# q and k parts stored once and doubled by a zero stride in the load; maxima without a lead of three buffers

## The chip, the cores and the metric

One core of one Trainium2 chip. The metric is the device time of one execution in microseconds (us); lower is better. The engines are named as in the profile: PE (matrix products; PEld is its weight load), DVE (vector), ACT (activation functions), POOL (GpSimd) and SP (the queue that issues most transfers). Transfers are issued by SP and ACT and carried by 16 DMA engines.

## The reference

The input is x of 8 batches x 1024 tokens x 256 features, float32. Three residual steps follow one another: half a mixture-of-experts layer, a causal attention of 16 heads of 16 features, and again half a mixture-of-experts layer.

```python
x = x + 0.5 * ffn(layernorm(x))
x = x + attn(layernorm(x))
x = x + 0.5 * ffn(layernorm(x))

# attn: q, k, v = projections of x with biases, 16 heads of 16
dots = einsum('bhid,bhjd->bhij', q * hd**-0.5, k)
dots = where(causal, -1e9, dots)
out = softmax(dots) @ v          # then @ Wo.T + bo

# ffn: two experts of 8 a token; an expert with more than cap = 1280 choices is dropped whole
keep = counts <= cap
```

An expert that more than 1280 of the 16384 choices fall on gives nothing. The kernel counts the choices, and runs the experts only where one is kept. In the executions shown none is: the profile is the attention with the routing's choices around it.

## The kernel before, in words

**Units.** The attention works in 32 units: 8 batches (`b`) x 4 groups of 4 heads (`g`). A unit's q and k lie in one of three tiles `qks[u % 3]`, of 128 rows: two heads of 64 rows each, for q and k (`t`) and for two pairs of heads (`pr`), 1024 tokens wide.

**Parts.** For float32 accuracy with products of a reduced type each head's q and k are split into a high and a low part of 16 rows. A head's 64 rows of q are high, low, high, low, those of k high, high, low, low, so one product of 64 rows sums all four combinations. `project(b, gp)` (lines 740 to 766) makes the parts for 8 heads: products `pq`, then on ACT `whole` and `high`, on POOL `low`, for each half of the tokens and for q and k. The tiles `high` and `low` have three buffers each. SP stores them into the DRAM tile `parts`; `fetch(u)` (lines 769 to 779) loads them from there into `qks`, for unit u + 2 while unit u runs. A batch has 8 such pairs of tiles.

**Maxima and scores.** `m_steps(u)` has 18 steps a unit, M: a product of q and k into PSUM (`sm`), and on DVE the row maxima (`mx`). They are needed before the scores. When all maxima of a half (`hf`) of the queries are there, `settle` turns them on DVE (`mxr`, `mneg`, `mside`), and `send` passes them through DRAM with two transfers of ACT's queue: `rows<-mside`, and after that has landed `neg<-rows`. `e_steps(u)` has 18 steps a unit, E: a product that starts with minus the maxima (`sc<-neg,take_m`), then k and q (`sc<-qk`), and ACT's exponential (`pT`). The first 5 E of a unit are of the first half of the queries, the other 13 of the second. POOL masks, and products with the values (`pav`) follow some steps later; their result is copied by ACT (`att`), and SP stores it (`sums<-att`), in the middle of the unit for the first half and a few steps into the next unit for the second. `sm` and `sc` share three pairs of PSUM banks.

**Order.** Every engine's instructions keep the order of the source (line 623 records each operation, so all have this line in the profile). A unit is 36 steps, E and M in turn: E of unit u, M of the units after it. A counter `count` tells the steps; `start(steps, lag)` (line 1229) puts work into `timed`, due `(3 * lag + 2) // 4` steps later, and `due()` runs it ahead of the step. So `fetch(u + 2, lag=6)`, started with a lag of 8, issues at steps 6, 11, 16 and 21 of unit u; `send` issues `rows` 2 steps after the last maxima of a half and `neg` 5 steps after that. In unit 1 three M are put ahead of the first E (lines 1307 to 1309), so from then on maxima run three M (six steps) ahead: the last M of a unit's own successor is done at step 29, and M at steps 31, 33 and 35 are already those of the unit after that. Between the steps `gap` lays in projections, values, the output product and the rest.

**Transfers.** Eight semaphores tell of the landings of all transfers of SP and ACT, by turns: in the built program each transfer waits for the landing of the eighth before it.

Of the kernel before, what the change touches and what calls it, by code (L numbers as in the profile page):

```python
# [10 lines left out]
F32 = mybir.dt.float32  # L11
# [18 lines left out]
def macaron_kernel(  # L30
# [24 lines left out]
    HD = D // NH  # L55
# [543 lines left out]
    def attention(run_no, src, dst, gate0, logits, tally):  # L599
# [4 lines left out]
        with stack:  # L604
# [134 lines left out]

            def project(b, gp):  # L740
                xnT = xnTs[b]
                parts = parts_d[b, gp] = passing.tile([2, 8, 4, HD, S], F32, tag=f"parts{gp}", name=f"parts{b}_{gp}")
                for s0 in range(0, S, 512):
                    for t, (wT, bT, scale) in enumerate(((wqT, bqT, QSCALE), (wkT, bkT, 1.0))):
                        pq = bank(f"pq{b}_{gp}_{s0}_{t}")
                        for o in (0, 256):
                            for c in range(DC):
                                product(
                                    pq[:, o : o + 256],
                                    wT[:, c, gp * P : (gp + 1) * P],  # L750
                                    xnT[:, c, s0 + o : s0 + o + 256],
                                    start=(c == 0),
                                    stop=(c == DC - 1),
                                )
                                if (c, o) != (DC - 1, 256):
                                    yield
                        whole = ap.tile([P, 512], F32, tag="whole", name=f"whole{b}_{gp}_{s0}_{t}")
                        high = ap.tile([P, 512], F32R, tag="high", name=f"high{b}_{gp}_{s0}_{t}", bufs=3)
                        low = ap.tile([P, 512], F32R, tag="low", name=f"low{b}_{gp}_{s0}_{t}", bufs=3)
                        on.scalar.activation(whole, pq, AF.Identity, bias=bT[:, gp : gp + 1], scale=scale)  # L760
                        on.scalar.copy(high, whole)
                        on.gpsimd.tensor_tensor(low.bitcast(F32), whole, high.bitcast(F32), ALU.subtract)
                        for c in range(4):
                            part = (high, low)[c // 2 if t else c % 2]
                            on.sync.dma_start(out=parts[t, :, c, :, s0 : s0 + 512], in_=part.bitcast(F32))
                        yield True


            def fetch(u, s0=0, w=S, lag=8):
                b, g = divmod(u, NG)  # L770
                gp, k = divmod(g, 2)
                for pr in range(2):
                    for t in range(2):
                        h = 4 * k + 2 * pr
                        on.sync.dma_start(
                            out=qks[u % 3][:, t, pr, s0 : s0 + w].bitcast(F32),
                            in_=parts_d[b, gp][t, h : h + 2].rearrange("h c d s -> (h c d) s")[:, s0 : s0 + w],
                        )
                        yield lag


# [49 lines left out]
            def m_steps(u):  # L831
# [56 lines left out]
                def settle(hf):  # L888
                    mx = ap.tile([P, 4, 2, 2], F32, tag="mxr", name=f"mxr{u}_{hf}")
                    on.vector.tensor_reduce(  # L890
                        mx.rearrange("p x b a -> p x a b"),
                        mx_tiles[u % 3][hf].rearrange("p h r (a b) s -> p (h r) a b s", a=2),
                        AX.X,
                        ALU.max,
                    )
                    yield
                    mx = mx.rearrange("p (h r) b a -> p h (r b a)", h=2)
                    neg = ap.tile([P, 2, 2, 8], F32R, tag="mneg", name=f"mneg{u}_{hf}")
                    high, low = neg[:, :, 0], neg[:, :, 1]
                    on.vector.tensor_scalar(high, mx, -1.0, None, ALU.mult)  # L900
                    yield
                    on.vector.scalar_tensor_tensor(
                        low.bitcast(F32), mx, -1.0, high.bitcast(F32), ALU.mult, ALU.subtract
                    )
                    yield
                    turned = ap.tile([P, 32], F32, tag="mside", name=f"mside{u}_{hf}")
                    on.vector.transpose(turned, neg.bitcast(F32).rearrange("p x c i -> p (x c i)"))
                    start(send(hf, turned), 3)
                    yield

                def send(hf, turned):
                    rows = passing.tile([8, 512], F32, tag="rows", name=f"rows{u}_{hf}")
                    on.scalar.dma_start(out=rows.rearrange("c (i s q) -> s c i q", i=4, s=4), in_=turned)
                    yield 6
                    on.scalar.dma_start(
                        out=negs[u % 2][hf][62:66, :, :512].bitcast(F32),
                        in_=rows.rearrange("(p r) s -> p r s", r=2),
                    )
# [310 lines left out]
            def start(steps, lag=0):  # L1229
                timed.append([count[0] + (3 * lag + 2) // 4, steps])  # L1230
# [29 lines left out]
            for u in range(-1, NU):  # L1260
                b, g = divmod(u, NG)
                rate, every = 17 / 12, FILLS
                if u < 0:
                    rate, every = 23 / 9, 2
                elif g == 0:
                    spare[0] = False
                    if b == 0:
                        work.append(project(0, 1))
                        rate = 8 / 3
                    if b + 1 < B:  # L1270
                        work += [enter(b + 1), project(b + 1, 0)]
                        if b:
                            work.append(leave(b - 1))
                        work += [project(b + 1, 1), values_of(b + 1)]
                    if b:
                        start(divide(b - 1, 1, 0), 4)
                        after[u - 1, 1] = divide(b - 1, 1, 1)
                    side.append(gate_first(b))
                elif g == 1 and b + 1 == B:
                    work.append(leave(b - 1))  # L1280
                elif g == 2:
                    if b + 2 < B:
                        start(read(b + 2), 24)
                    if b + 1 == B:
                        start(divide(b, 0, 0), 12)
                        start(divide(b, 0, 1), 16)
                        after[u, 0] = divide(b, 1, 0, 4, (8, 1, 6, 8))
                elif g == 3:
                    if b + 1 < B:
                        start(divide(b, 0, 0), 8)  # L1290
                        start(divide(b, 0, 1), 20)
                    if b + 2 < B:
                        side.appendleft(prepare(b + 2))
                    if b + 1 == B:
                        after[u - 1, 1] = divide(b, 1, 1, 4, (6, 1, 4, 5))
                        last_on.append(ap.tile([P, 4, P], F32, tag="wsb", name="last_on", bufs=4))
                        on.gpsimd.memset(last_on[0], 0.0)
                        rate = 8 / 3
                if u == 0:
                    start(fetch(2, lag=5), 26)  # L1300
                elif u >= 0 and u + 2 < NU:
                    start(fetch(u + 2, lag=6), 8)
                if u < 0:
                    for _ in range(18):
                        step(maxima, every, rate, 1)
                else:
                    if u == 1:
                        for n in range(3):
                            step(maxima, every, rate, n)
                    es = deque(e_steps(u))  # L1310
                    for k, which in enumerate("EMEMEM" * 6):
                        small = 3 if k % 6 in (1, 5) else 0
                        if which == "E":
                            step(es.popleft(), 2 if u + 1 == NU else every, rate, 0 if u + 1 < NU else 2)
                        elif stream[0] < 18 * NU:
                            step(maxima, every, rate, small)
                if u < 0:
                    while 0 not in bases:
                        take(work)
                elif g == NG - 1:  # L1320
                    while work and u + 1 < NU:
                        drain(work.popleft())
# [75 lines left out]
```

## Time and profile before

| what | value |
|---|---|
| median of 3 runs | 1232.97 us (1225.27 to 1233.84) |
| the profiled execution's own time | 1243.32 us |
| its span | 1241.2 us |
| PE, DVE, ACT, POOL busy | 92%, 76%, 60%, 35% |
| PE busy in 96 to 1168 us | 1033.7 of 1072 us |
| DMA moved | 190.25 MB, mean 153 GB/s |
| loads `qk<-parts` | 124 of 512 KB, 8 of 256 KB |
| stores `parts<-high`, `parts<-low` | 128 and 128 of 256 KB |
| `rows<-mside`, `neg<-rows` (ACT's queue) | 64 and 64 of 16 KB |

The span is that of one profiled execution; its own time lies 10.3 us above the median of the runs. The page gives busy times of each engine, the DMA queues, the chain of work that ended last and the costliest groups of instructions. "Idle" is told with what ended it; "issue" in the chain is time for which the profile shows no wait. The table of windows gives, for a stretch, the busy time of each engine, the granted clock of PE, the mean busy share of the 16 DMA engines and GB/s.

### The profile page before, as it was taken

The page shows a single profiled execution, that of the slowest core. Times are in us where ns is not written, and L with a number is a line of the kernel's source. Part 1 is how long each engine was busy: PE and PEld are TensorE (multiplying, and loading weights), DVE is VectorE, ACT ScalarE, POOL GpSimd, SP SyncE. Part 2 cuts the span into 40 slices and gives each one's busy share as a digit, 9 for nine tenths or more (in the row PEclk, how much of TensorE's full clock was granted, in tenths as well). Part 3 has the DMA queues.
Part 4 walks back from the last instruction along what each step waited for, and adds up shares of the span by engine and source line. Part 5 has one row for each costly group of instructions (what it writes and reads, how often), then busy time and mean ns, then how long its engine had stood idle before and what let it go on. Part 6 is the DMA issues. An engine that isn't in the chain of part 4 may idle for free.

```text
span 1241.2 us, 36200 instructions
## 1 busy us (share of the span) xinstructions
PE 1143.7 (92%) x15178; PEld 668.6 (54%) x15178; DVE 939.9 (76%) x1649; ACT 739.6 (60%) x955; POOL 434.8 (35%) x773
## 2 busy tenths in 40 slices
PE   4698999999999998999899998999989999999982
PEld 2455555555565554655456555655546555555541
DVE  2487668878698777888688787988778886798923
ACT  3155676666576565675566655765656655665650
POOL 2434233343344233442334433342344413232331
PEclk9698999999899998999999999999999999999997
DMA  3634674363555545353653635555553545543201
GB/s 108 234 123 167 208 224 130 119 231 105 189 153 158 187 153 189 119 182 134 214 168 112 221 112 194 148 161 189 164 192 113 185 137 182 156 126 105 83 19 38
DMA packets 108501, 190.25 MB, mean 153 GB/s; under 512 B 24736, under 2 KB 42280, under 8 KB 108328
## 3 DMA queue, kind: packets, MB, share of 16 engines
q1 hardware_dynamic: 96776, 184.54, 45.6%
q10 hardware_dynamic: 11552, 3.29, 1.2%
q8 instruction: 122, 2.00, 0.6%
q14 instruction: 51, 0.42, 0.1%
HBM read 94.50 MB, written 93.31 MB: 151 GB/s over the span
## 4 chain that ended last, share of the span: by engine, by line
PE 79%; DVE 10%; DMA 4%; issue 3%; ACT 2%; POOL 1%; ACTq 0%; SPq 0%; POOLq 0%; DVEq 0%
PE sc L623 23%; PE pav L623 21%; PE sm L623 16%; PE pq L623 8%; DVE mx L623 7%; PE px L623 4%; PE pv L623 4%; DMA rows<-mside 3%; PE pta L623 2%; ACT pT L623 1%; DMA parts<-low 1%; DVE mneg L623 0%; DVE st_a L623 0%; DVE xn_a L623 0%; DMA qk<-parts 0%
## 5 line engine op out<-in xcount | busy, mean ns | idle before, releaser
L623 DVE TENSOR_REDUCE mx<-sm 128x2 f32<-128x1024 f32 (+2 forms) x576 | 685.2, 1216 | 211.9 <-PE sm L623 186.0
L623 ACT ACTIVATE pT<-sc 128x1024 f32<-128x1024 f32 x576 | 575.0, 1023 | 329.7 <-PE sc L623 284.6
L623 POOL TENSOR_SCALAR_AFFINE_SELECT pT<-pT 128x256 f32<-128x256 f32 (+1 forms) x448 | 190.7, 440 | 496.0 <-ACT pT L623 485.4
L623 PE MATMUL pav<-pT,vaug 128*32 128x256 f32 (+3 forms) x4608 | 325.8, 390 | 1.4 <-ACT att L623 1.4
L623 PE MATMUL sm<-qk 64*128 64x512 f32 (+3 forms) x1536 | 266.9, 385 | 38.3 <-issue 20.7
L623 PE MATMUL sc<-neg,take_m 64*128 64x512 f32 x1152 | 266.8, 459 | 6.9 <-DVE mx L623 3.5
L623 PE MATMUL sc<-qk 64*128 64x512 f32 (+3 forms) x1536 | 230.9, 337 | 0.0
L623 PEld LDWEIGHTS sm<-qk 64*128 64x128 f32 x1536 | 142.1, 189 | 139.1 <-issue 69.8
L623 PEld LDWEIGHTS pav<-pT,vaug 128*32 128x32 f32 x4608 | 113.6, 109 | 103.4 <-issue 54.7
L623 PEld LDWEIGHTS sc<-neg,take_m 64*128 64x128 f32 x1152 | 110.5, 188 | 100.4 <-issue 50.3
L623 PEld LDWEIGHTS sc<-qk 64*128 64x128 f32 x1536 | 147.6, 188 | 16.5
L623 POOL TENSOR_TENSOR low<-whole,high 128x512 f32<-128x512 f32 x64 | 82.0, 1281 | 157.1 <-ACT high L623 146.2
L623 PE MATMUL sm<-masked,before_k 64*128 64x128 bf16 (+1 forms) x1280 | 87.2, 215 | 0.0
L623 PE MATMUL pq<-xnT,wkT 128*32 128x256 f32 x1024 | 75.7, 405 | 0.0
L623 PE MATMUL px<-woT,on 128*32 128x264 f32 x1024 | 73.7, 387 | 0.9 <-ACT on L623 0.9
L623 PE MATMUL pv<-wvT,xnT 128*32 128x264 f32 x1024 | 74.0, 391 | 0.0
L623 PE MATMUL pq<-xnT,wqT 128*32 128x256 f32 x1024 | 72.7, 389 | 0.5 <-ACT xnT L623 0.5
L623 PEld LDWEIGHTS <-before_k 64*128 64x128 bf16 x1280 | 38.3, 97 | 43.8 <-issue 27.5
L623 POOL TENSOR_TENSOR x_a<-x_a,bo_all 128x512 f32<-128x512 f32 x32 | 41.5, 1301 | 57.5 <-DVE xn_a L623 36.5
L623 PE MATMUL pta<-ident,xn_a 128*32 128x128 f32 (+1 forms) x912 | 33.9, 278 | 18.3 <-DVE xn_a L623 18.1
L623 PEld LDWEIGHTS pq<-xnT,wkT 128*32 128x32 f32 x1024 | 34.4, 115 | 28.0 <-issue 10.8
L623 PEld LDWEIGHTS pq<-xnT,wqT 128*32 128x32 f32 x1024 | 33.2, 112 | 27.8 <-issue 10.8
(128 smaller groups left out, 734.3 us busy)
## 6 DMA issues: line engine op xcount, KB each, us to landing
qk<-parts SPq DMA_DIRECT2D x124, 512.0 KB
parts<-high SPq DMA_DIRECT2D x128, 256.0 KB
parts<-low SPq DMA_DIRECT2D x128, 256.0 KB
sums<-att SPq DMA_DIRECT2D x62, 256.0 KB
x_a<-in_L_attn_x_dram SPq DMA_DIRECT2D x16, 512.0 KB
out_dram<-x_a SPq DMA_DIRECT2D x16, 512.0 KB
on<-sums SPq DMA_DIRECT2D x30, 256.0 KB
rs<-inv SPq DMA_DIRECT2D x30, 256.0 KB
```

The lines of the kernel that those rows point to most:

```text
L623: i = call(*args, **kwargs)
```

## The change

Three things change. The DRAM tile `parts` holds each head's high and low part once (32 rows a head, not 64). A load reads them twice by a stride of zero: for q the 32 rows (high, low of a feature side by side) as a block twice over, for k each of the 32 rows twice in a row; a load takes one head, so there are 8 loads a unit, two at each of the four steps. And the three M ahead in unit 1 go, with shorter lags of `send` for the last unit.

```diff
-                parts = parts_d[b, gp] = passing.tile([2, 8, 4, HD, S], F32, ...)
+                parts = parts_d[b, gp] = passing.tile([2, 8, 2 * HD, S], F32, ...)
...
-                        for c in range(4):
-                            part = (high, low)[c // 2 if t else c % 2]
-                            on.sync.dma_start(out=parts[t, :, c, :, s0 : s0 + 512], in_=part.bitcast(F32))
+                        form = ("h (d c) s -> c h d s", "h (c d) s -> c h d s")[t]
+                        for c, part in enumerate((high, low)):
+                            on.sync.dma_start(
+                                out=parts[t].rearrange(form, c=2)[c, :, :, s0 : s0 + 512], in_=part.bitcast(F32)
+                            )
...
                 for pr in range(2):
                     for t in range(2):
-                        h = 4 * k + 2 * pr
-                        on.sync.dma_start(
-                            out=qks[u % 3][:, t, pr, s0 : s0 + w].bitcast(F32),
-                            in_=parts_d[b, gp][t, h : h + 2].rearrange("h c d s -> (h c d) s")[:, s0 : s0 + w],
-                        )
+                        for h in range(2):
+                            rows = parts_d[b, gp][t, 4 * k + 2 * pr + h][:, s0 : s0 + w]
+                            on.sync.dma_start(
+                                out=qks[u % 3][64 * h : 64 * h + 64, t, pr, s0 : s0 + w].bitcast(F32),
+                                in_=rows.unsqueeze(t).to_broadcast([2 * HD, 2, w] if t else [2, 2 * HD, w]),
+                            )
                         yield lag
...
-                    start(send(hf, turned), 3)
+                    start(send(hf, turned), 3 if u + 1 < NU else 1)
...
-                    yield 6
+                    yield 6 if u + 1 < NU else 4
...
-                    if u == 1:
-                        for n in range(3):
-                            step(maxima, every, rate, n)
```

In the built program a store of q has 128 rows at one stride and 512 elements (before: 8, 16 and 512), one of k still 8, 16 and 512. A load of q reads 2 (stride zero), 32 and 1024 elements, one of k 32, 2 (stride zero) and 1024, both into 64 rows of the tile.

More of the change, by code (lines that the diff above doesn't have):

```diff
@@ L741, in project @@
                 xnT = xnTs[b]
-                parts = parts_d[b, gp] = passing.tile([2, 8, 4, HD, S], F32, tag=f"parts{gp}", name=f"parts{b}_{gp}")
+                parts = parts_d[b, gp] = passing.tile([2, 8, 2 * HD, S], F32, tag=f"parts{gp}", name=f"parts{b}_{gp}")
                 for s0 in range(0, S, 512):
```

## The prediction

> **What bounds the kernel now.** I read the page first: which engine is full, and what the chain that ended last is made of.
>
> ```profile
> PE 1143.7 (92%) x15178; PEld 668.6 (54%) x15178; DVE 939.9 (76%) x1649; ACT 739.6 (60%) x955; POOL 434.8 (35%) x773
> ...
> q1 hardware_dynamic: 96776, 184.54, 45.6%
> ...
> PE 79%; DVE 10%; DMA 4%; issue 3%; ACT 2%; POOL 1%; ACTq 0%; SPq 0%; POOLq 0%; DVEq 0%
> ```
>
> PE is busy 92% of the span and is 79% of the chain. The 16 DMA engines are half idle on average; as long as transfers land in time they cost nothing. So the change, which moves only transfers and the order of maxima, can cost or gain only where PE waits for a transfer. Next, how many of the 16 DMA engines one transfer uses: the table of windows (busy times, granted clock, busy share of the DMA engines, GB/s), in a stretch that holds stores of parts alone and one that holds loads of 128 rows.
>
> ```profile
> 28.50:30.50 2.00, 0.58 (x12) 0.09 (x4) 0.00 (x0) 1.02 (x3) 1.26 (x1) 1.00 0.51 183
> ...
> 57.00:61.00 4.00, 3.93 (x50) 1.65 (x46) 4.00 (x4) 0.88 (x4) 1.31 (x3) 1.00 0.99 383
> ```
>
> With several stores queued, 0.51 of the engines work: eight. Such a store's pattern in DRAM is 8 heads, 16 rows, 512 elements. With loads whose slowest dimension is 128 rows, all 16 work, at 383/(0.99 x 16) = 24.2 GB/s each; over the whole span the page gives 184.54 MB/(0.456 x 16 x 1241.2 us) = 20.4. The number of engines follows the slowest dimension of a pattern.
>
> Then the timeline of one unit, from its first score (PE) to the first score that reads the second half's maxima, and two of ACT's pairs of transfers.
>
> ```profile
> 291.01 0.50 PE L623 MATMUL sc<-neg,take_m 64*128 64x512 f32 x2
> ...
> 296.73 0.32 SPq L623 DMA_DIRECT2D sums<-att  x1
> ...
> 297.62 1.72 SPq L623 DMA_DIRECT2D qk<-parts  x2
> ...
> 300.23 0.40 PE L623 MATMUL sc<-neg,take_m 64*128 64x512 f32 x2
> ```
> ```profile
> 321.20 0.53 ACTq L623 DMA_DIRECT2D rows<-mside  x1
> ...
> 330.36 0.63 ACTq L623 DMA_DIRECT2D neg<-rows  x1
> ...
> 340.60 0.54 ACTq L623 DMA_DIRECT2D rows<-mside  x1
> ...
> 345.55 0.65 ACTq L623 DMA_DIRECT2D neg<-rows  x1
> ```
>
> SP issues the next loads as soon as the sums that wait for att are out, 6 to 8 us into the unit; the score that needs the second half's neg comes 9.2 us into it. The transfer neg cannot be issued before rows has landed. From the increments of each transfer's semaphore in the trace, rows lands in 1.9 us when nothing of SP is outstanding, 6.6 us after 321.20 with six of SP's transfers ahead; neg in 2.1 us, and 4.6 to 6.4 us with five ahead. It lands just before the last of those that SP issued ahead of it: ACT's transfers queue behind SP's and overtake about one.
>
> Last, the chain in order of time shows the one place where a load is late today.
>
> ```profile
> 323.37 1.03 ACT pT L623
> 324.40 1.91 issue
> 326.31 0.93 PE sm L623 x6
> ```
>
> PE stands until a maximum of the unit after next gets its q and k (that load lands at 326.2). The same step recurs at 470.15 (2.64), 615.17 (2.78), 759.77 (2.39), 903.50 (2.64) and 1048.47 (1.10): 13.5 us in all. It comes back every 144.5 us, four units of 36 steps each: 36.1 us a unit, about 1 us a step.
>
> **The change, part by part.**
>
> *Stores.* Each projection tile is stored with 2 transfers, not 4: 128 instead of 256 of 256 KB, 33.5 MB less. Those of q now have 128 equal rows (16 engines), those of k still 8 heads. SP saves 128 issues of some 0.6 us and pays 132 more of 0.46 us for the loads; SP waits most of the time, so both count nothing.
>
> *Loads.* A unit has 8 of 256 KB, not 4 of 512 KB, issued in pairs at the same four steps (6, 11, 16, 21). Those of k have slowest dimension 32 in the source, 64 in the tile: 16 engines, 0.7 us, as before. Those of q read [2 copies, 32 rows, 1024]. No row shows a slowest dimension of 2. Bounds: all 16 engines, 262144 B/(16 x 24.2) = 0.7 us; or two engines, 131072 B/24.2 = 5.4 us each. The nearest row is the store (8 of 8), so I take two engines: a pair of q occupies them for 10.8 us, and every other transfer that has a share on these two waits.
>
> The Trainium skill, DMA: Bandwidth & Descriptors, section Rules for kernel authors, says that an outermost zero-stride broadcast of c copies confines a DMA to at most c engines, and speaks against just this pattern; by it the load takes the 5.4 us, and the opposite end would need it to be wrong. The window with 0.51 agrees with it for a count of 8; no row here shows 2.
>
> Is there room? On the busiest two engines: q loads 33.5 MB/2 = 16.8 MB; k loads 2.1, stores 1.05 + 2.1, sums 1.0, on and rs 2.0, x in and out 1.05, small ones 0.4: 26.5 MB. At 24.2 GB/s 1096 us, at 20.4 1300 us; the stretch that carries loads lasts some 1140 us. They are full, or just over: queues of 5 to 15 us behind each pair.
>
> *Who waits: neg of the second half.* Without the lead the last maximum of a unit comes 6 steps later, so its rows goes out at step 2 of the next unit and its neg at step 7, where it went out at step 1. SP's pair of q, issued at 6 to 7 us, is then just ahead of it; it is needed at 9.2 us. Lower bound, overtaking all: issue 7.3 + 2.1 = 9.4, a wait of 0.2 us. Upper bound, behind both q: 6.5 + 10.8 + 1 = 18, less one overtaken transfer at most: a wait of 7 us. I take 3 us (one q of 5.4 overtaken, one not: landing near 12.3). PE's queue is in order, so maxima, values and projections behind that score stand too. 31 units x 3 = +93 us.
>
> *Who waits: ACT for rows of the first half.* Its rows goes out at step 16, with the second pair of q, and its neg is queued on ACT at step 21: ACT stands until rows has landed, and behind it the exponentials, for which PE waits after some 3 steps (three pairs of PSUM). Rows of 2 us: nothing. Rows of 9 to 10 us, behind both q: ACT stands 4.5 us, PE 2.5. I take 1 us x 31 = +31 us.
>
> *The lead.* The maxima of unit u+2 start at step 37 after the step counter's zero of unit u, not 31; the last load goes out at 21. Even at 10 us a pair q and k are there by 36. The 13.5 us above go: between 0 and -13.5, I take -10. If the q loads were later by another 5 us, this cover would be gone and the wait would come back as 1 to 5 us a unit.
>
> *Start and end.* At the start the first maxima wait for POOL's memset until 53 us, but the loads of units 0 and 1 now put 4 x 2.7 x 2 + 4 x 5.4 = 43 us on two engines, with rows of unit 0 behind them: 0 to +20, I take +10. In the last unit no maxima lie between the scores; lags shortened by 2 each: 0 to +8, I take +2.
>
> Sum: 93 + 31 - 10 + 10 + 2 = +126. The profiled execution's own time was 1243.3 us (span 1241.2), 10.3 above the median of 1233.0 of the runs shown. 1243.3 + 126 - 10.3 = **1359 us**.
>
> **Rivals.** (a) ACT's transfers interleave with SP's packet by packet: neg is late by 0.5 us, rows (32 small packets an engine between packets of 4 KB) still blocks ACT for about a microsecond: 31 x 1.5 - 13 + 8 + 2 = +44, 1277 us. For it: some neg land at 2.1 us with one transfer ahead. Against it: 4.6 to 6.4 with five. The same page of the Trainium skill, section Queues, rings and completion order, has the engines take turns between the queues of SP and ACT at every packet; by it the sum would be this one, by the rows here it is nearer the next, and the measured 6.4 us decides for me.
> (b) Strict order: 7 + 2.5 us a unit, 31 x 9.5 - 13 + 20 + 4 = +306, 1538 us. For it: six transfers ahead and 6.6 us. Against: the last one is mostly overtaken, and as PE stands the next pair comes later, which thins the queue.
> (c) Faster: the repeated copies are spread over 16 engines after all. Then a q load lands in under 3 us, 33.5 MB less are written, the 13.5 us go, and the waits for rows on the chain (2.8% of the span, 35 us) shrink by a third: 1243.3 - 13 - 12 - 10.3 = 1208 us. It decides as soon as a pair of q takes under about 3 us. For it only that no row shows the pattern; against it the window with 0.51.
> (d) No change: neg and q arrive within the idle time there is, since 8% of PE is idle; but of its 97.5 us 29.2 lie ahead of 96 us and 30.0 after 1168 us, by windows over these stretches; the 1072 us between have 38.3, in hundreds of small gaps.
>
> **How the numbers follow.** Forecast 0.46, (a) 0.24, (b) 0.20, (c) 0.05, (d) 0.05. A measurement of this kernel tells about 1% from no change. Faster by over 1% is (c): 0.05; within 1% (d): 0.05; slower the rest: 0.90. The forecast's own range is 1300 to 1430 (1 to 5 us a unit around its terms); with (a) below and most of the way to (b) above, 1255 to 1520.
>
> **What would show it.** Right: in a stretch with q loads alone the share of DMA engines is near 2/16; scores of the second half wait for neg (PE or its weight load ahead of sc, idle of some us once a unit); neg on ACT issued over 5 us after rows; the waits of 1.9 to 2.8 us of sm gone. Wrong: a pair of q landing within 3 us; PE at 92% or more; or PE waiting chiefly for qk (loads later than I have them) or ACT for high (stores holding its three buffers).

## The result and the profile after

| | before | after |
|---|---|---|
| median (6 runs each, same chip) | 1233.4 us (1225.3 to 1237.2) | 1427.5 us (1420.9 to 1431.7) |
| profiled execution, its span | 1243.3, 1241.2 us | 1425.8, 1424.0 us |
| PE busy, PE idle within the span | 1143.7, 97.5 us | 1212.1, 211.9 us |
| mean granted clock of PE | 0.964 | 0.917 |

The changed kernel takes 1.158 times as long, 95% interval 1.153 to 1.163: slower, as forecast, by 195 us where the forecast had 126. The page of the profile after, with the lines that answer to those shown of before:

```profile
span 1424.0 us, 36302 instructions
...
PE 1212.1 (85%) x15178; PEld 702.3 (49%) x15178; DVE 937.4 (66%) x1649; ACT 738.2 (52%) x955; POOL 433.4 (30%) x773
...
q1 hardware_dynamic: 80144, 150.99, 34.3%
...
PE 50%; DMA 31%; DVE 9%; issue 3%; ACT 2%; SPq 2%; POOL 1%; ACTq 1%; POOLq 0%; DVEq 0%
DMA qk<-parts 15%; PE sc L623 15%; PE pav L623 14%; PE sm L623 9%; DMA neg<-rows 9%; DVE mx L623 5%; PE pq L623 5%; DMA rows<-mside 3%; PE pv L623 3%; PE px L623 2%; DMA parts<-low 2%; DMA rs<-inv 2%; SPq L623 2%; ACT pT L623 2%; PE pta L623 1%
```

33.5 MB less pass through q1 and the transfers are busy for a smaller share, yet DMA is now 31% of the chain that ended last; it was 4%. The chain goes through the loads `qk` (15%) and `neg` (9%). What PE waits for (line, what ended the wait, us in total, times, longest):

```profile
PE sc L623 <- DMA neg<-rows: 79.9, 22, 6.1
PE sm L623 <- ACT pT L623: 33.4, 12, 5.4
PE sc L623 <- DVE mx L623: 20.7, 14, 7.5
PE sm L623 <- DMA qk<-parts: 18.7, 6, 8.7
...
PE sm L623 <- issue: 5.9, 2, 3.5
```

In before the same answer has 3.5 us for `mx`, and:

```profile
PE sm L623 <- issue: 20.7, 7, 4.1
...
PE sm L623 <- DMA qk<-parts: 12.3, 3, 10.7
...
PE sm L623 <- ACT pT L623: 4.5, 4, 2.1
...
PE sc L623 <- DMA neg<-rows: 1.7, 1, 1.7
```

Now one unit in the timeline of after (start, duration, engine, and in brackets the idle time with what ended it). The unit starts at 506.1.

```profile
507.81 0.53 ACTq L623 DMA_DIRECT2D rows<-mside  x1
...
511.93 0.49 PE L623 MATMUL sc<-neg,take_m 64*128 64x512 f32 x2
...
512.12 0.34 SPq L623 DMA_DIRECT2D sums<-att  x1
...
512.55 2.48 SPq L623 DMA_DIRECT2D qk<-parts  x4
...
512.88 0.63 ACTq L623 DMA_DIRECT2D neg<-rows  x1
...
521.38 0.80 PE L623 MATMUL sc<-neg,take_m 64*128 64x512 f32 x2 [5.73 <-DMA neg<-rows]
```

SP issues q, q, k, k behind `sums`; ACT issues `neg` 0.33 us after the first of them. By the increments of its semaphore `neg` lands at 521.25, 8.4 us after its issue, where it takes 2.1 alone; the two loads of q land at 523.3 and 528.2. PE starts 0.13 us after `neg`, 5.73 us late, and its two products of that line then take 0.80 us, where they took 0.49. The table of windows for the end of this stretch:

```profile
516.00:520.50 4.50, 0.00 (x0) 0.00 (x0) 0.92 (x1) 0.00 (x0) 0.97 (x3) 0.90 0.30 112
521.50:527.00 5.50, 5.50 (x48) 3.17 (x50) 1.22 (x1) 1.44 (x2) 1.08 (x4) 0.56 0.13 52
```

First line: PE does nothing for 4.5 us. Second: only the loads of q are under way, the share of the DMA engines is 0.13, two of 16, at 52 GB/s, which is 5.0 us for a load of q. And the clock granted to PE is 0.56: after it has stood it is busy all the time, but at little more than half speed.

Over all units the order on the queues makes the difference. In 13 units `neg` of the second half was issued up to 1.1 us behind the first load of a pair of q (in one of them at the same moment); it landed 5.6 to 8.6 us later, median 7.8. In 7 units it went out 0.2 to 2.0 us ahead of the pair, and landed in 2.2 to 5.8 us. In 9 units the pair of q came 2.5 us or more after `neg`; it then landed in a median of 2.1 us (2.1 to 5.6).

### The profile page after: what moved, and what is told of

The parts are those of the page before. It is cut to its first block, busy times and chain, and to the rows that moved or that the text cites. A ratio compares the mean times of both kernels' runs of the same rounds, so it can differ in the third digit from the quotient of the medians.

```text
span 1424.0 us, 36302 instructions
## 1 busy us (share of the span) xinstructions
PE 1212.1 (85%) x15178; PEld 702.3 (49%) x15178; DVE 937.4 (66%) x1649; ACT 738.2 (52%) x955; POOL 433.4 (30%) x773
## 4 chain that ended last, share of the span: by engine, by line
PE 50%; DMA 31%; DVE 9%; issue 3%; ACT 2%; SPq 2%; POOL 1%; ACTq 1%; POOLq 0%; DVEq 0%
DMA qk<-parts 15%; PE sc L623 15%; PE pav L623 14%; PE sm L623 9%; DMA neg<-rows 9%; DVE mx L623 5%; PE pq L623 5%; DMA rows<-mside 3%; PE pv L623 3%; PE px L623 2%; DMA parts<-low 2%; DMA rs<-inv 2%; SPq L623 2%; ACT pT L623 2%; PE pta L623 1%
## 5 line engine op out<-in xcount | busy, mean ns | idle before, releaser
L623 PE MATMUL sc<-neg,take_m 64*128 64x512 f32 x1152 | 277.5, 477 | 104.7 <-DMA neg<-rows 79.9
L623 PE MATMUL pav<-pT,vaug 128*32 128x256 f32 (+3 forms) x4608 | 344.8, 408 | 1.4 <-ACT att L623 1.4
L623 PE MATMUL sm<-qk 64*128 64x512 f32 (+3 forms) x1536 | 280.4, 397 | 59.3 <-ACT pT L623 33.4
L623 PEld LDWEIGHTS sm<-qk 64*128 64x128 f32 x1536 | 155.4, 199 | 170.3 <-ACT pT L623 77.9
L623 PE MATMUL sc<-qk 64*128 64x512 f32 (+3 forms) x1536 | 238.3, 346 | 0.0
L623 PEld LDWEIGHTS sc<-qk 64*128 64x128 f32 x1536 | 153.5, 194 | 14.6
L623 PE MATMUL sm<-masked,before_k 64*128 64x128 bf16 (+1 forms) x1280 | 93.8, 221 | 0.0
L623 PE MATMUL pq<-xnT,wqT 128*32 128x256 f32 x1024 | 81.3, 418 | 0.5 <-ACT xnT L623 0.5
L623 PEld LDWEIGHTS px<-woT,on 128*32 128x32 f32 x1024 | 34.0, 116 | 35.0 <-issue 16.5
L623 PEld LDWEIGHTS pv<-wvT,xnT 128*32 128x32 f32 x1024 | 33.6, 117 | 34.1 <-issue 13.3
```

What stands on the lines that cost most here:

```text
L623: i = call(*args, **kwargs)
```

## The experiments

All were timed against before on the same chip. Differences between kernels of different chips are taken from the ratios, in parts of 1233 us. "Idle" is the span less PE's busy time, both of the page; the next two columns are PE's waits `sc` for `neg` and `sm` for ACT's `pT`.

| kernel | median us | ratio to before (95%) | idle | PE busy | clock | neg | pT |
|---|---|---|---|---|---|---|---|
| before | 1233.4 | | 97.5 | 1143.7 | 0.964 | 1.7 | 4.5 |
| after | 1427.5 | 1.158 (1.153 to 1.163) | 211.9 | 1212.1 | 0.917 | 79.9 | 33.4 |
| split | 1233.3 | 0.996 (0.993 to 0.999) | 84.7 | 1151.6 | 0.969 | 26.0 | 0 |
| split_lead | 1197.1 | 0.967 (0.962 to 0.973) | 68.1 | 1127.4 | 0.980 | 1.7 | 1.0 |
| lead_off | 1306.4 | 1.056 (1.050 to 1.063) | 136.0 | 1167.2 | 0.948 | 67.5 | 0.4 |
| once_lead | 1502.6 | 1.215 (1.208 to 1.223) | 267.1 | 1228.2 | 0.897 | 1.8 | 142.9 |
| dose2 | 1399.4 | 1.135 (1.129 to 1.141) | 192.8 | 1203.8 | 0.929 | 57.6 | 42.2 |
| dose4 | 1278.2 | 1.034 (1.025 to 1.043) | 117.2 | 1167.1 | 0.957 | 32.6 | 20.3 |
| k_first | 1401.2 | 1.135 (1.130 to 1.141) | 204.4 | 1200.7 | 0.930 | 24.1 | 73.9 |
| late3 | 1418.8 | 1.154 (1.146 to 1.161) | 204.6 | 1213.4 | 0.922 | 60.7 | 57.5 |
| lead_late5 | 1652.0 | 1.339 (1.332 to 1.345) | 386.5 | 1272.7 | 0.861 | 4.0 | 87.5 |
| half0 | 1412.9 | 1.146 (1.142 to 1.150) | 213.3 | 1197.1 | 0.917 | 93.3 | 55.5 |
| half1 | 1260.6 | 1.021 (1.018 to 1.024) | 108.7 | 1159.3 | 0.963 | 30.5 | 4.8 |
| tidy | 1194.5 | 0.969 (0.964 to 0.974) | 67.6 | 1124.6 | 0.980 | 1.8 | 0 |

The theory: a load of q on two engines holds up ACT's small transfers that go out beside it, and PE waits for these. Rivals: the loss comes from the missing lead; from the stride of zero itself, not the count of engines; or the two engines are full, so that everything waits wherever it is put.

**split: the repeated stride taken out of q alone.** Each load of q becomes two of 32 rows, on 16 engines; k, storage and the missing lead stay as in after.

```diff
-    out=qks[u % 3][64 * h : 64 * h + 64, ...], in_=rows.unsqueeze(0).to_broadcast([2, 2 * HD, w])
+    for r in (64 * h, 64 * h + 32):
+        on.sync.dma_start(out=qks[u % 3][r : r + 32, ...], in_=rows)
```

> The changed kernel, but each q load is made as two loads of 32 rows without a repeated stride (12 loads a unit, not 8; the same bytes). Theory: all 16 engines carry them, the queue ahead of neg and rows is gone and so is most of the loss: 1225 to 1275 us, PE's wait for neg under 20 us in all. Rival (eight or more issues a unit cost, or the stride of zero itself): no faster than the changed kernel, 1420 us or more.

Measured 1233.3 us; by the ratios 200 us (16.2% of before) less than after. One access pattern of one group of loads carries the loss, and the inner stride of zero of k costs nothing that shows.

**split_lead: the same with the lead.** split with the three maxima ahead and the old lags of `send`.

```diff
+                    if u == 1:
+                        for n in range(3):
+                            step(maxima, every, rate, n)
```

> The same with the three maxima ahead put back. Theory: parts are stored once, so half of the stores are gone, all loads are carried by 16 engines: as fast as before or a little faster, 1205 to 1240 us. Rival (issues cost): over 1260 us.

1197.1 us, 36 less than split, and a little below what was expected. So the change is three things: storing once with loads on 16 engines gains 40 us (before to split_lead), taking the lead away costs 36 (split_lead to split), the loads on two engines cost 200 (split to after): together the 195.

**lead_off: only the lead taken out of before.** Edit: the last two hunks of the change, in before.

> The kernel before, with the three maxima ahead in unit 1 taken away (and the lags of the last unit shortened as in the change); stores and loads of parts as before. Theory: the lost time comes from q loads that two DMA engines carry, and the lead alone is worth little: neg then goes out at step 7 and lands 2.1 us later while loads take 1.3 us each, a wait of under 1 us a unit, against 13.5 us of late loads saved: 1225 to 1260 us. Rival (the lead is what is missed, whatever the loads): 31 units x 3 to 5 us, 1330 to 1400 us.

1306.4 us, between the two expectations; both missed.

```profile
PE sc L623 <- DMA neg<-rows: 67.5, 24, 5.6
PE sm L623 <- DMA qk<-parts: 15.0, 3, 11.2
```

With the storage of before, without the lead, `neg` is late as well, 24 times. Nothing runs on two engines here; but stores run on eight. The lead is worth 69 us with before's storage and 36 with split's: what stands around `neg` on the queues sets the price. That it is the stores and not the larger loads was not tried.

**once_lead: the lead put back into after.** Edit: as in split_lead, in after.

> The changed kernel with the three maxima ahead put back: q loads still read a leading stride of zero. Theory: two engines still carry q, so most of the loss stays; neg goes out 6 steps earlier, ahead of the pair of q loads, which saves its waits (98 us of PE's idle time in the changed kernel), but the maxima then want the loads 6 steps earlier: 1330 to 1420 us. Rival (the lead is what is missed): near 1235 us.

1502.6 us, slower than after by 71: my expectation had the wrong sign. (The 98 us that it gives for the wait for `neg` in after, and k_first's too, are 79.9 by the view shown above.) The waits of PE, and the chain by line:

```profile
PE sm L623 <- ACT pT L623: 142.9, 38, 8.3
```
```profile
DMA rows<-mside 21%; PE sc L623 12%; PE pav L623 11%; PE sm L623 9%; DMA qk<-parts 8%; DMA parts<-low 5%; DVE mx L623 4%; PE pq L623 4%; ACT pT L623 4%; DMA x_a<-in_L_attn_x_dram 3%; DMA inv<-few 3%; PE px L623 3%; PE pv L623 2%; ACTq L623 2%; PE pta L623 1%
```

`neg` is in time again (1.8 us). But with maxima six steps earlier `rows` of the first half goes out just behind a load of q: in 28 of 32 units one was issued within the 3 us ahead of it. ACT, whose next instruction is `neg`, stands until `rows` has landed (median 12 us from `rows` to `neg`, 5.7 in before), the exponentials stand behind it, and `sm` finds no free PSUM. The wait has gone from `neg` to `rows`.

**dose2 and dose4: two and four engines without a stride of zero.** As split, but the 32 rows of q lie in DRAM as 2 blocks of 16 (4 of 8) with one unused row after each, so that the slowest dimension of a load is 2 (4) and every stride is above zero.

```diff
-    parts = passing.tile([2, 8, 2 * HD, S], ...)
+    parts = passing.tile([2, 8, 2, 17, S], ...)      # dose4: [2, 8, 4, 9, S]
...
-    in_=rows                                         # 32 rows at one stride
+    in_=parts_d[b, gp][0, h][:, :16]                 # dose4: [:, :8]
```

> As the kernel with each q load made as two loads of 32 rows without a repeated stride (1233 us), but the rows of q lie in DRAM as two blocks of 16 with a row left free after each, so that the slowest dimension of a load is 2. Theory (the slowest dimension decides how many engines carry a load): two engines again, 1400 to 1450 us, like the changed kernel, without any stride of zero in q. Rival (the repeated stride, or reading rows twice, is what costs): 1225 to 1245 us.

> The same with four blocks of 8 rows, a free row after each: slowest dimension 4. Theory: four engines carry q loads, a pair occupies them for half the time (5.4 us instead of 10.8): between 1233 and 1425, nearer the fast end, 1270 to 1330 us. Rival (all that counts is 16 or not 16): near 1425. Rival (stride of zero): 1225 to 1245 us.

1399.4 and 1278.2 us: the second is as expected, the first a hair under its range, and the rival, the stride itself, falls as the main cause. The time goes with the number of engines that a load of q gets: 1233 at 16, 1278 at 4, 1399 at 2. This is the rule that the prediction took from the Trainium skill, DMA: Bandwidth & Descriptors, Rules for kernel authors, now with a slowest dimension of 2 that repeats nothing. The direct sight of it in after is the window above with its share of 0.13; by the packets in the traces, exactly two are under way in 36% of the time from 96 us to 75 us before the end in after, and in 34% in dose2. By the ratios dose2 is still 28 us faster than after; its q comes in loads of half the size, and what these 28 us are was not tried.

**k_first: the pairs change places.** After with the pair of k at steps 6 and 16, that of q at 11 and 21.

```diff
-                    for t in range(2):
+                    for t in (1, 0):
```

> The changed kernel with the loads of k ahead of those of q in each pair of heads. The two busy engines carry the same bytes. Theory (what counts is what SP has issued just ahead of ACT's neg): neg of the second half, issued within a microsecond of the first load, has only k ahead of it, and PE's wait for it falls from 98 to under 40 us: 1320 to 1380 us. Rival (the two engines are simply full, whatever the order): 1410 to 1440 us.

1401.2 us, only 28 less than after; 1320 to 1380 was expected.

```profile
PE sm L623 <- ACT pT L623: 73.9, 23, 6.2
...
PE sc L623 <- DMA neg<-rows: 24.1, 16, 4.0
```
```profile
ACT pT L623 <- DMA rows<-mside: 110.9, 21, 7.5
```

The wait for `neg` did fall, from 79.9 to 24.1, as the theory says. But now `rows` of the first half stands behind the pair of q, which is mostly issued 4 to 9 us ahead of it (second fence, ACT's waits), and the wait for ACT rises from 33.4 to 73.9.

**late3 and lead_late5: the loads later in the source.** After with the loads at steps 9, 14, 19, 24; once_lead with them at 11, 16, 21, 26.

```diff
-                    start(fetch(u + 2, lag=6), 8)
+                    start(fetch(u + 2, lag=6), 12)   # lead_late5: 15
```

> The changed kernel with the loads of unit u + 2 issued three steps later (steps 9, 14, 19, 24 instead of 6, 11, 16, 21); same transfers, same bytes, same two engines a load of q. Theory (the order on the queues decides: neg of the second half, issued at step 7, and rows of the first half, at step 16, stand right behind a pair of q): neg now goes out ahead of the first pair, rows two steps ahead of the second. The waits of sc for neg (79.9 us) fall under 20 us, those of sm for ACT under 20 us, and the time falls to 1240 to 1310 us. Rival (the two busiest engines are full, 26.5 MB, and whatever is issued waits for them wherever it stands): 1370 to 1430 us, with the waits moved to the loads (sm for qk).

> The changed kernel with the three maxima ahead put back and the loads issued five steps later (steps 11, 16, 21, 26), so that with the lead too rows of the first half (step 10) stands ahead of the first pair of q and neg of the second half (step 1) behind nothing. Theory (order): against 1502.6 us for the lead with the loads at steps 6 to 21, the waits of sm for ACT (142.9 us) fall under 40 us; the time is 1230 to 1320 us, with some us a unit of sm for qk, as the last loads come at step 26 and are read from step 31 on. Rival (full engines): 1430 to 1510 us.

1418.8 and 1652.0 us. The theory's numbers fail for both. Late3 falls into the range of the rival (full engines), but its timeline shows that the edit did only in part what it was for:

```profile
499.59 0.53 ACTq L623 DMA_DIRECT2D rows<-mside  x1
...
503.90 0.34 SPq L623 DMA_DIRECT2D sums<-att  x1
...
504.34 1.14 SPq L623 DMA_DIRECT2D qk<-parts  x2
...
504.65 0.63 ACTq L623 DMA_DIRECT2D neg<-rows  x1
...
511.93 0.80 PE L623 MATMUL sc<-neg,take_m 64*128 64x512 f32 x2 [4.49 <-DMA neg<-rows]
```

From `rows` to the first load of q it is 4.75 us; in after, at 507.81 and 512.55, it was 4.74. A step is a place in the source, not a time. In such a unit nothing that waits stands between `sums` and the loads on SP's queue: three steps later in the source, SP issues them at the same moment, as soon as `sums` is out. In other units they did move; over all, the pair is issued up to 1.1 us ahead of `neg`, or with it, in 10 units, where it was 13, and the wait for `neg` fell from 79.9 to 60.7 us while that of `sm` for ACT rose from 33.4 to 57.5. So late3 neither proves nor refutes. Lead_late5, slower than both expectations, has a wait of its own on top:

```profile
PE sm L623 <- DMA qk<-parts: 190.0, 31, 10.1
```

Maxima wait for the loads 31 times, 6.1 us on average: with the lead they are read from step 31 on, and loads of 8 to 19 us (median 14) issued up to step 26 are not there.

**half0 and half1: one pair of q on two engines, the other split.** After late3 it was still open whether the order on the queues decides or the fill of the two engines (in after, by the packets in the trace, exactly two engines work in 36% of the time from 96 us to 75 us before the end, and none in only 6%). Both kernels take the same bytes off the two engines. In half0 the pair of step 6 keeps the repeated stride, in half1 that of step 16.

```diff
-                            if t:
+                            if t or pr == 0:             # in the loads of split; half1: pr == 1
```

> The changed kernel in which only the first pair of q loads of a unit (step 6) keeps the repeated stride outermost; the second pair (step 16) is four loads of 32 rows on 16 engines. Half of the bytes of q leave the two engines. Theory (the two engines are full: in the changed kernel some DMA engine works 94% of the steady stretch, and moving the loads only moved the wait): with 8 MB less of a load of 26.5 MB the backlog is gone by the next pair; neg, still right behind the pair of step 6, waits less than in the changed kernel (PE sc for neg 30 to 55 us, not 79.9), and the time is 1260 to 1310 us. Rival (the order at neg decides, whatever the load): neg waits the same 70 to 85 us, only the waits for rows go, and the time is 1340 to 1380 us.

> The mirror image: only the second pair of q loads (step 16), with rows of the first half right behind it, keeps the repeated stride outermost; the pair of step 6, which neg of the second half stands behind, is split. Theory (full engines): about the time of its mirror image, 1250 to 1300 us, as the same bytes are gone. Rival (the order at neg decides): PE's wait for neg falls below 30 us as in the wholly split kernel, and the time is 1235 to 1275 us, at least 60 us below its mirror image. If the wait for rows were the larger one, it would be above its mirror image.

1412.9 and 1260.6 us, 152 us apart with the same bytes on the same engines. The waits of PE in half0, then in half1:

```profile
PE sc L623 <- DMA neg<-rows: 93.3, 23, 6.1
PE sm L623 <- ACT pT L623: 55.5, 15, 7.0
```
```profile
PE sc L623 <- DMA neg<-rows: 30.5, 18, 3.8
PE sm L623 <- DMA qk<-parts: 11.1, 5, 5.7
```

Full engines, which the expectations call the theory here, fall: with half the load gone from the two engines half0 is within 15 us of after, and `neg` with the pair beside it still lands 7.0 to 8.8 us after its issue. It is slower than even the number given for "the order at neg decides", 1340 to 1380, since the wait of `sm` for ACT did not go with the second pair but rose to 55.5 us. ACT itself stands 54.6 us there until loads `qk` land (37.9 in after). ACT reads no `qk`; each transfer that it issues waits for the landing of the eighth before it. But the landings in the trace of half0 show that this is only the end of the wait. One unit:

```profile
462.78 0.53 ACTq L623 DMA_DIRECT2D rows<-mside  x1
...
476.91 0.65 ACTq L623 DMA_DIRECT2D neg<-rows  x1
```

The pair of step 6 was issued from 457.44 on and lands at 469.2 and 475.5; `rows` of the first half, 5.3 us behind it, lands at 474.8, and `neg` follows 2.1 us later, when the eighth transfer before it, a load of k, has landed. So it is in all 14 units in which PE waits over 1 us for ACT: the pair was issued 5 to 11 us ahead of `rows`, `rows` lands 8.1 to 12.0 us after its issue, and the eighth transfer adds 0.2 to 2.2 us. The same pair of step 6 thus holds up `neg` of the second half where it is beside it, and else `rows` of the first half behind it. Half1 is in the range of the other side, 1235 to 1275, with 30.5 us of waits for `neg` against 93.3, and 30 us above split by the ratios. So what decides is which small transfer stands beside or shortly behind a pair, not the fill of the engines: the pair of step 6 costs 185 us over split (half0), that of step 16 only 30 (half1).

**tidy: a version from what the runs show.** q is stored doubled, in the order in which a load has one stride; k once, doubled by its inner stride of zero; every store has 128 rows at one stride, loads are 4 of 512 KB as in before, and the lead stays.

```diff
+    n = 2 if t else 4
+    form = parts[t].rearrange("h (d c) s -> c h d s", c=n)
+    for c in range(n):
+        part = (high, low)[c % 2]
+        on.sync.dma_start(out=form[c, :, :, s0 : s0 + 512], in_=part.bitcast(F32))
...
+    rows = parts_d[b, gp][t][h : h + 2].rearrange("h r s -> (h r) s")[:, s0 : s0 + w]
+    on.sync.dma_start(out=qks[u % 3][:, t, pr, s0 : s0 + w].bitcast(F32),
+                      in_=rows.unsqueeze(1).to_broadcast([4 * HD, 2, w]) if t else rows)
```

> A version by what the runs so far point to: q stored doubled (4 stores a pair of tiles), k once (2 stores), rows laid out so that every store has 128 rows at one stride; loads as before, 4 of 512 KB a unit, k doubled by an inner stride of zero; three maxima ahead. Theory: every transfer on 16 engines with few issues: 1190 to 1210 us, like the kernel with split q loads and the lead (1197), or a little under it. Rival (the 8 loads and more were needed to spread the work): over 1220 us.

1194.5 us, 3.1% below before (2.7 to 3.6): as expected, and faster than both kernels; split_lead is level with it. The chain of tidy:

```profile
PE 82%; DVE 13%; POOL 2%; issue 2%; ACT 1%; DMA 0%; POOLq 0%; ACTq 0%; DVEq 0%
```

DMA, 4% in before and 31% in after, is gone from it. It moves 167.8 MB through q1, 16.8 more than after: bytes were not the price.

## Why the prediction was right, and where its sum was short

**q on two engines: right.** The share of 0.13 in the window with q alone, and dose2. The pair lands 10.4 and 15.3 us after 512.88, not within 3 us; rival (c) falls, and so does (d). What (c) would have given is seen in split, which has its 16 engines and the missing lead: 1233 us against its 1208, as `neg` is late there too, by 26.0 us in all.

**neg, 31 x 3 = 93 us: the size held, its make-up did not.** Measured 79.9 us, 22 times, so 3.6 us on average. But it is not 3 us in each unit: in the 13 units with the pair of q just ahead it is 2.7 to 6.1 us, 62 us together, and in seven of the nine where the pair comes 2.5 us later it is nothing. That the sum came near is partly luck. Nor does `neg` land between the two loads, as the forecast had it: in those 13 units it lands 1.9 to 5.4 us ahead of the first. Rival (a), with `neg` late by 0.5 us in each, and rival (b), 7 us in each, both fall by the same line.

**ACT for rows, 31 us: the size right, the pair wrong.** `sm` for `pT` went from 4.5 to 33.4, +29, and `rows` of the first half took 6.6 to 10.9 us in the units that make up nearly all of it. But the prediction put it behind the second pair of q (step 16). In after that pair is issued 0.4 us behind `rows` or later in the units with the longest of these waits, and the first pair, of step 6, 4 to 5 us ahead of it. Half1, with the second pair alone on two engines, has 4.8 us of this wait, half0, with the first alone, 55.5. So that this term came out is luck. The median from `rows` to `neg` of the first half rose from 5.7 to 6.8 us; that of the second stayed at 5, so the sign "issued over 5 us after" which the prediction gave told nothing there.

**The lead, -10: about right as a wait, wrong as the lead's worth.** "issue" and `qk` ahead of `sm` together went from 33.0 to 24.6 us. But the lead's whole worth, with `neg` in it, is 36 us (split to split_lead), and in after putting it back costs 71: it decides which small transfer meets the loads.

**Not in the sum: maxima.** `sc` waits 20.7 us for `mx`, +17, which the prediction had not; what makes `mx` late was not tried.

**Start, +10: about right.** PE does 540 instructions in the first 96 us, 716 in before; 176 at 0.074 us (1033.7 us for 13956 in before's middle) are 13 us. Only 4 of them are idle time (33.3 us there against 29.2); the others are slower products, at a clock of 0.75 against 0.88.

**What the sum lacked: "+126 on 1243.3" counted PE's waits alone and kept its busy time.** The waits were right in total: idle time rose by 211.9 - 97.5 = 114 us. But the same 15178 products took 68 us longer, 1212.1 against 1143.7. From the forecast to the median: 1359 + 68 (busy) - 12 (waits 114, not 126) + 10 (the 10.3 between profiled execution and median taken off, which after did not repeat) + 2 (its profiled execution lies 1.7 below its median) = 1427. So one term is missing, with half the size of the rest; most of it is PE's clock. The clock records of both traces hold only 1.0 and 0.5, so by the means PE had half speed for 2 x (1 - 0.964) x 1241 = 89 us in before and for 2 x 0.083 x 1424 = 236 us in after. It was busy in 58 and in 174 us of these; half of the difference, 58 us, is the most that the clock can account for, and what the other 10 are is open. That 1427 still lies within 1300 to 1430 is luck: this range was made for other lengths of the waits, not for slower products. The table has it for every kernel: tidy, with the fewest waits, has 0.980 and 1124.6 us of work; lead_off 0.948 and 1167.2; lead_late5 0.861 and 1272.7. The Trainium skill, TensorE: Matmul & The Clock Gate, section HAM oscillation, says that a wait for a transfer of more than some 3.4 us makes the matrix engine run at half clock for a while after it. The timeline agrees with the outcome (5.73 us of standing, then 0.56 and 0.80 us instead of 0.49); where the threshold lies no run here shows. The row that could have told me was in the windows of before, a clock of 0.88 in the first 96 us, where PE is busy for 66.8, against 0.98 in the middle:

```profile
0.00:96.00 96.00, 66.81 (x716) 38.49 (x716) 48.63 (x85) 32.18 (x58) 36.02 (x66) 0.88 0.47 155
```

## What to carry to other kernels

Look at the slowest dimension of every transfer's pattern before its bytes: here 33.5 MB were saved and 195 us lost, and the same doubling cost nothing as an inner stride (k), or as two loads. A small transfer that something waits for must not go out beside a long one on few engines, or shortly behind it, and moving either in the source may do nothing if its queue has no wait in between: look in the trace at what was issued in the 10 us ahead of it. Where PE will wait for several microseconds at a time, put about half on top of the waits (here 114 us of idle time brought 68 us of slower products, 60%; over the kernels of the table with over 30 us more idle time than before it is 45 to 65%).

## What the hardware showed unexpectedly

- A transfer of ACT's queue of 16 KB that takes 2.1 us alone takes a median of 7.8 us when SP issues a pair of loads on two engines of which the first is up to 1.1 us ahead of it; the second may come 0.3 us after it. It then lands 1.9 to 5.4 us (median 2.5) before the first of the pair. If the pair comes 2.5 us later, 2.1 us is the median.
- The cost of waits isn't additive: the second pair of q on two engines costs 30 us where the first is split (half1 over split), and 15 where it is not (after over half0).
- PE's idle time and its busy time rise together. From tidy to lead_late5 idle rose by 319 us and, with the same products, busy time by 148.
